# First layer of a two-layer adaLN model: retention in the planned instruction order, in groups of four batches with a choice of tokens each

## The chip, the cores and the metric

The kernel runs on one core of a Trainium2 chip (trn2). The metric is the device time of one execution in microseconds (us). A core has five engines that each take their instructions in program order: PE (TensorE, matrix products; PEld is its weight load), DVE (VectorE), ACT (ScalarE, with tables for its functions), POOL (GpSimd) and SP (SyncE, which here only issues DMA transfers; ACT and POOL issue some too). They meet through semaphores. Tensors lie in on-chip memory of 128 partitions; products go to PSUM, eight banks of 128 x 512 f32. All arithmetic here is in f32.

## What is computed

Input x is 16 batches of 256 tokens with 128 channels. Each of two layers has an attention-like part and a mixture of experts, each modulated by vectors that come from `silu(c) @ wmod`:

```python
h = layernorm(x) * (1 + ca) + sa
x = x + ga * retention(h)        # layer 0; layer 1: selective scan, then layer norm
h = layernorm(x) * (1 + cb) + sb
x = x + gb * experts(h)          # layer 0: experts choose tokens; layer 1: tokens choose 2 of 8
```

Retention has 8 heads of 16 channels with one decay each: a state `S = g*S + k v^T` and outputs `q S` over the 256 tokens, a group norm over each head and all tokens, weight and bias, and a projection `Wo`. The experts of layer 0 choose: a softmax over 8 experts for each token, then for each batch and expert the 64 tokens of highest probability; two products (128 to 512, exact gelu, 512 to 128), times the probability, added back to the tokens. Layer 1 has a selective scan with 256 inner channels and 16 states each, and then experts of width 448 in which a token goes to its best two.

## The kernel before

**Front, in Tile's own order (L334 to L713).** Tile is the layer that allocates tiles, puts in the waits, and here also orders the instructions of each engine. `attention(g)` (L418 to L494) takes batches 4g to 4g+3: layer norm of the inputs (`ln_stats` L334 with a Sqrt on ACT L344 and a reciprocal on DVE L345, `ln_apply` L349 on DVE), a transpose and modulation to hT, q and k with heads split in even and odd (ke, ko), v, the state S of the first 128 tokens, and scores in four PSUM banks of the pool `ps_sc`, four heads' rows each (L470). DVE multiplies each bank by the decay matrix into `pr0` to `pr3`, two buffers each (L472); PE forms the outputs from them (L481, L485), ACT copies them to yT, DVE takes their statistics (L493). `finish_attention(g)` (L496 to L528) does the group norm: two small products that average over a head, Sqrt, reciprocal, the normalized yn on DVE with its bias added on POOL (L521, L522), the projection, gate, and sum into X (L528). `gate(g)` (L530 to L545) normalizes X and forms the scores of the experts for all tokens. The calls are `attention(0)`, setup of layer 1's weights (L550 to L672), then for each g `attention(g+1)`, `finish_attention(g)`, `gate(g)`. After group 3 one choice serves all 16 batches (L681 to L713): softmax; the transpose to rows, one for each batch and expert, 128 in all; eight rounds of `max` and `match_replace`, eight tokens each (L700, L701); a running sum that numbers the chosen tokens; a write of these rows to memory (`spd`, L709); and a transpose back to `slot_tok`.

**The rest, in a planned order.** The class `Plan` holds chains of instructions, each with an urgency (a smaller number goes first), and prices of instructions. Its `issue` goes through a simulated time of its own, takes for each engine what could begin first (within 0.15 us, the most urgent), and binds the order with dependences between successive instructions of an engine. Chains name what they `need` and tokens that they `take` and `give` (buffers). All of these instructions are recorded under L115. Experts of layer 0 go by quarters q of four batches: `gather(b)` (urgency -10+q; builds one-hot matrices gg from slot_tok, px gathers tokens), `hidden(q)` (-8+q; ph, then gelu to hg), `outputs(q)` (-9+q; pye, ysb) and `scatter(q)` (-9+q; reads the rows of spd back, spread over partitions, as gt and pr, makes weights gt from them, pos adds back to X). q = 0 uses for ph four PSUM banks (dA0, dA1, c, y) that the scans use later. Layer 1 follows: `front(b)` (-16), `gates(b)` (-14), `scans()`, `back(k)` (-15), and `second()`, which plans the experts of layer 1, once all batches have left layer 0. `scans` works in 256 units of 128 x 512: `rep` rows come back from memory (dd) spread over partitions by SP, three buffers; ACT makes dA, POOL makes dB (twelve buffers), DVE scans into h and multiplies into dB, PE sums. Its chains have urgency -20 but for DVE's, 5. The experts of layer 1 (`expert` L1338 on, products pa and pg in L1372, py in L1402; sl is formed on DVE) go in tiles.

The memory of the retention (`p0`, `at`) is released before the pools `ml` (rep, dB) and `rf` (layer 0's experts) are opened.

Of the kernel before, what the change touches and what calls it, by code (L numbers as in the profile page):

```python
# [18 lines left out]
P = 128  # L19
# [239 lines left out]
def adaln_two_layers(ctx: ExitStack, tc: tile.TileContext, a: dict, out: bass.AP):  # L259
# [7 lines left out]

    def fixed32(pool, shape, name):
        return pool.tile(shape, U32, tag=name, name=name)
# [11 lines left out]
    early = ExitStack()  # L281
    pe = early.enter_context(tc.tile_pool(name="pe", bufs=1))
    pk0 = fixed(pe, [P, 554], "pk0")
# [13 lines left out]
    def w0(k):  # L297
        return pk0[:, PK0[k][0] : PK0[k][1]]

# [3 lines left out]
    with tc.tile_pool(name="su", bufs=1) as su, tc.tile_pool(name="sups", bufs=2, space=PSUM) as sups:  # L303
# [4 lines left out]
        nc.scalar.activation(sc.rearrange("p l b -> p (l b)"), w0("c"), AF.Silu)  # L308
# [20 lines left out]


# [3 lines left out]
    def ln_stats(srcs, rs=None):  # L334
        n = len(srcs)
        st = sm.tile([P, n, 6], F32, tag=f"st{n}", name="st")
        mv = sm.tile([P, n, 2], F32, tag=f"mv{n}", name="mv")
        sd = sm.tile([P, n], F32, tag=f"sd{n}", name="sd")
        rs = sm.tile([P, n], F32, tag=f"rs{n}", name="rs") if rs is None else rs
        for i, s in enumerate(srcs):  # L340
            nc.vector.bn_stats(st[:, i, :], s)
        for i in range(n):
            nc.vector.bn_aggr(mv[:, i, :], st[:, i, :])
        nc.scalar.activation(sd, mv[:, :, 1], AF.Sqrt, bias=eps5)  # L344
        nc.vector.reciprocal(rs, sd)  # L345
        return mv, rs

    def ln_apply(o, s, mv, rs, i):
        nc.vector.tensor_scalar(o, s, mv[:, i, 0:1], rs[:, i : i + 1], ALU.subtract, ALU.mult)  # L349

    def modulate(o, s, l, which, b):

        nc.scalar.activation(
            o, s, AF.Identity,
            bias=mods[l][:, 2 * which, b : b + 1], scale=mods[l][:, 2 * which + 1, b : b + 1],
        )

# [3 lines left out]

# [7 lines left out]
    spd = dr.tile([P, 2 * L], F32, tag="spd", name="spd", bufs=1)  # L369
# [3 lines left out]
    with tc.tile_pool(name="p0", bufs=1) as p0:  # L373
        c0 = fixed(p0, [P, 1536], "c0")
        eo = fixed(p0, [P, 2], "eo")
        nc.scalar.dma_start(c0, a["c0"][:, 0:1536])
        nc.scalar.dma_start(eo, a["c0"][:, 1600:1602])
        nc.scalar.dma_start(iota0, a["c0"][:, 1536:1600])
        nc.scalar.dma_start(lcol, a["c0"][:, 1602:1603])
        for b in range(4, B):  # L380
            nc.sync.dma_start(X[b], xsrc[b])
        nc.sync.dma_start(fw1, a["fw1"].rearrange("p (e h) -> p e h", e=E))
        nc.sync.dma_start(fw2, a["fw2"].rearrange("p (e h c) -> p e h c", e=E, h=4))

        def k0(k):
            return c0[:, C0[k][0] : C0[k][1]]

        dec = k0("dec").rearrange("p (j n) -> p j n", j=4)
        even, odd = eo[:, 0:1], eo[:, 1:2]


        wveo = fixed(p0, [P, 2, D], "wveo")
        nc.gpsimd.memset(wveo, 0.0)
        wv4 = w0("wv").rearrange("p (j q e) -> p j q e", q=2, e=DH)
        for par in range(2):
            nc.gpsimd.tensor_copy(
                wveo[:, par, :].rearrange("p (j q e) -> p j q e", q=2, e=DH)[:, :, par, :], wv4[:, :, par, :]
            )

        with tc.tile_pool(name="su1", bufs=1) as su1, tc.tile_pool(name="at", bufs=2) as at, tc.tile_pool(name="yt", bufs=8) as ytp, tc.tile_pool(  # L400
            name="ps_sc", bufs=4, space=PSUM
        ) as ps_sc, tc.tile_pool(name="ps_w", bufs=3, space=PSUM) as ps_w, tc.tile_pool(
            name="ps_g", bufs=1, space=PSUM
        ) as ps_g:
            p_tok = at.tile([P, NCH, B, E], F32, tag="p_tok", name="p_tok", bufs=1)
            gs = ps_g.tile([P, NCH, B, E], F32, tag="gs", name="gs")

            def transposed(xn, l, which, b, name):
                pt = ps_w.tile([P, 512], F32, tag="w", name=f"ptr_{name}{b}")
                for ch in range(NCH):  # L410
                    nc.tensor.transpose(pt[:, ch * P : (ch + 1) * P], xn[:, ch, :], ident)
                hT = at.tile([P, L], F32, tag="hT", name=f"hT_{name}{b}")
                modulate(hT, pt[:, :L], l, which, b)
                return hT

            yTs, gst, tabs = {}, {}, {}

            def attention(g):  # L418

                bs = range(4 * g, 4 * g + 4)  # L420
                tabs[g] = at.tile([P, 4, D], F32, tag="tab0", name=f"tab0_{g}")
                nc.sync.dma_start(tabs[g], rowd0[4 * g : 4 * g + 4, 0:D].unsqueeze(0).to_broadcast([P, 4, D]))
                mv, rs = ln_stats([X[b][:, ch, :] for b in bs for ch in range(NCH)])
                gst[g] = sm.tile([P, 4, 2], F32, tag="gst", name=f"gst{g}")
                for i, b in enumerate(bs):
                    xn = at.tile([P, NCH, D], F32, tag="xna", name=f"xna{b}")
                    for ch in range(NCH):
                        ln_apply(xn[:, ch, :], X[b][:, ch, :], mv, rs, NCH * i + ch)
                    hT = transposed(xn, 0, 0, b, "a")
                    pqk = ps_w.tile([P, 2, L], F32, tag="w", name=f"pqk{b}")  # L430
                    nc.tensor.matmul(pqk[:, 0, :], w0("wq"), hT, start=True, stop=True)
                    nc.tensor.matmul(pqk[:, 1, :], w0("wk"), hT, start=True, stop=True)
                    q = at.tile([P, L], F32, tag="q", name=f"q{b}")
                    ke = at.tile([P, L], F32, tag="ke", name=f"ke{b}")
                    ko = at.tile([P, L], F32, tag="ko", name=f"ko{b}")
                    nc.scalar.copy(q, pqk[:, 0, :])  # L436
                    nc.vector.tensor_scalar(ke, pqk[:, 1, :], even, None, ALU.mult)
                    nc.scalar.activation(ko, pqk[:, 1, :], AF.Copy, scale=odd)
                    qd = at.tile([P, P], F32, tag="qd", name=f"qd{b}")
                    nc.gpsimd.tensor_tensor(qd, q[:, P:L], k0("qdec"), ALU.mult)  # L440

                    pv = ps_w.tile([P, NCH, 2 * D], F32, tag="w", name=f"pv{b}")
                    for ch in range(NCH):
                        nc.tensor.matmul(
                            pv[:, ch, :], hT[:, ch * P : (ch + 1) * P], wveo.rearrange("p q d -> p (q d)"),
                            start=True, stop=True,
                        )
                    v = at.tile([P, NCH, 2 * D], F32, tag="v", name=f"v{b}")
# [107 lines left out]
            def k1(k):  # L556
                return pk1[:, PK1[k][0] : PK1[k][1]]
# [1004 lines left out]
```

## Time and profile before

| what | value |
|---|---|
| median of 3 runs | 1448.89 us (1442.01 to 1449.62) |
| profiled execution, its own time | 1455.8 us, clock 0.833 |
| its span | 1453.8 us, 19595 instructions |
| busy: PE, DVE, ACT, POOL | 1042.1 (72%), 921.6 (63%), 732.0 (50%), 729.3 (50%) us |
| first and last scan | 384.9 and 1198.8 us |
| chain that ended last, by engine | PE 32%, DVE 25%, ACT 14%, issue 9%, POOL 9%, DMA 6% |

How to read the views: the slices cut the span in 40 equal parts (36 us) with the busy share of an engine in tenths, and PEclk, the clock granted to PE. A table by stretch has the stretch, its length, then for PE, PEld, DVE, ACT and POOL the busy us with the number of records, then the granted clock, the share of DMA and GB/s. The lines of waits say which engine and tile waited for which, with the us in total, the number of times, and the longest. A group of one tile's instructions gives the shortest, median and longest duration in ns, and the first and the last start. The chain goes back from the last instruction, at each step to what released it; its lines are start, us, what. "<-" stands between output and inputs of an instruction, or between a waiting instruction and what it waited for.

### The profile page before, as it was taken

The numbers are of one execution on the slowest core, as the hardware profiler recorded it, in microseconds if no ns is written. First come the engines' busy times: TensorE is split into PE (matmuls) and PEld (weight loads), VectorE is DVE, ScalarE is ACT, GpSimd is POOL, SyncE is SP. The second block draws the span as 40 slices with busy tenths as digits, with TensorE's granted clock in tenths as the row PEclk, the third lists the DMA queues.
The fourth block names the chain that finished last, engine by engine and source line by source line (L and its number), as shares of the span: only waits on it lengthen the run. The fifth ranks groups of instructions, "written<-read, shape, count | busy, mean of one in ns | idle before, by whom it ended". The sixth has DMA issues, their size and how long they took to land.

```text
span 1453.8 us, 19595 instructions
## 1 busy us (share of the span) xinstructions
PE 1042.1 (72%) x6090; PEld 708.8 (49%) x6090; DVE 921.6 (63%) x1783; ACT 732.0 (50%) x1538; POOL 729.3 (50%) x1062
## 2 busy tenths in 40 slices
PE   5897795598878786768745576587627788778780
PEld 3575574386646554445423244254414455556560
DVE  3555555532497989888968688878926883423340
ACT  1222121333678977867655466767514654334441
POOL 0002203001566866757877787858673872322535
PEclk9996886699998988998965697778869979889895
DMA  7060000324345834476483343454323531112322
GB/s 255 6 169 8 9 1 0 76 48 109 102 116 143 192 87 137 110 159 167 131 235 110 102 128 92 104 131 118 93 83 89 125 94 44 36 46 53 80 64 54
DMA packets 105429, 142.01 MB, mean 98 GB/s; under 512 B 15560, under 2 KB 83584, under 8 KB 104704
## 3 DMA queue, kind: packets, MB, share of 16 engines
q1 hardware_dynamic: 99792, 124.84, 33.0%
q0 software_dynamic: 4256, 9.18, 2.3%
q10 hardware_dynamic: 1280, 6.74, 1.6%
q8 instruction: 51, 0.84, 0.3%
q14 instruction: 50, 0.41, 0.1%
HBM read 114.60 MB, written 26.12 MB: 97 GB/s over the span
## 4 chain that ended last, share of the span: by engine, by line
PE 32%; DVE 25%; ACT 14%; issue 9%; POOL 9%; DMA 6%; SPq 2%; another core or an unknown queue 2%; DVEq 0%; POOLq 0%; ACTq 0%
DVE h L115 10%; DVE dB L115 5%; PE py L1402 4%; ACT L115 4%; PE pa L1372 3%; ACT dA L115 3%; PE pg L1372 3%; POOL dB L115 3%; PE pxs L115 2%; PE pm L115 2%; DVE pr L472 2%; PE pye L115 2%; DVE sl L115 2%; DMA rep<-dd 2%; PE ph L115 2%
## 5 line engine op out<-in xcount | busy, mean ns | idle before, releaser
L115 POOL TENSOR_TENSOR dB<-rep,bt 128x512 f32<-128x512 f32 x256 | 327.7, 1303 | 149.6 <-DMA rep<-dd 96.3
L115 DVE TENSOR_TENSOR_SCAN h<-dA,dB 128x512 f32<-128x512 f32 x256 | 314.6, 1229 | 54.4 <-ACT dA L115 33.3
L115 ACT ACTIVATE dA<-rep,A 128x255 f32<-128x255 f32 x512 | 241.4, 476 | 149.5 <-DVE h L115 138.3
L115 DVE TENSOR_TENSOR dB<-h,ct 128x512 f32<-128x512 f32 x256 | 176.1, 688 | 6.5
L1402 PE MATMUL py<-w,mT 112*128 x680 | 102.3, 298 | 36.0 <-ACT mT L115 19.2
L115 DVE SCALAR_TENSOR_TENSOR sl<-sl,pa 128x448 f32<-128x448 f32 x85 | 52.4, 616 | 119.3 <-ACT sl L115 101.4
L1402 PEld LDWEIGHTS py<-w,mT 112*128 112x128 f32 x680 | 92.6, 206 | 64.9 <-issue 30.7
L1372 PE MATMUL pa<-w,xT 128*128 x170 | 93.0, 632 | 37.5 <-issue 19.1
L115 POOL DMA_INDIRECT got<-ydr,pos x64 | 61.4, 960 | 106.7 <-DMA xt<-disp 53.2
L115 PE MATMUL ya<-dB,c 128*32 128x512 f32 x512 | 82.4, 763 | 39.8 <-DVE dB L115 39.8
L115 ACT ACT_TABLE_LOAD x70 | 89.8, 1283 | 2.1 <-issue 0.9
L1372 PE MATMUL pg<-w,xT 128*128 x170 | 86.8, 595 | 2.7 <-DVE sl L115 1.0
L440 POOL TENSOR_TENSOR qd<-q,c 128x128 f32<-128x128 f32 x16 | 7.3, 457 | 159.2 <-ACT q L436 148.3
L115 PE MATMUL ph<-xin,fw 128*128 128x256 f32 x256 | 70.2, 417 | 23.6 <-DVE ysb L115 8.1
L1323 POOL DMA_INDIRECT disp<-hs,pos x64 | 61.9, 968 | 40.9 <-DVE pos L115 22.4
L115 ACT ACTIVATE yt<-py 128x128 f32<-128x128 f32 x85 | 23.3, 274 | 105.2 <-PE py L1402 52.5
L115 PE MATMUL pxs<-hTm,wcv 128*128 128x256 f32 x256 | 76.0, 445 | 0.0
L115 ACT COPY mT<-pm 112x512 f32<-112x512 f32 x85 | 49.3, 584 | 46.7 <-PE pm L115 33.6
L115 PE MATMUL pye<-fw,hg 128*64 128x128 f32 x1024 | 66.8, 283 | 6.0 <-ACT hg L115 5.9
L115 PE MATMUL pm<-c,sl 128*112 128x128 f32 x340 | 59.3, 299 | 14.0 <-issue 7.9
L115 PEld LDWEIGHTS ph<-xin,fw 128*128 128x128 f32 x256 | 50.4, 207 | 38.4 <-ACT xin L115 9.0
L115 PEld LDWEIGHTS pye<-fw,hg 128*64 128x64 f32 x1024 | 59.0, 141 | 19.2 <-ACT hg L115 8.3
(284 smaller groups left out, 2155.6 us busy)
## 6 DMA issues: line engine op xcount, KB each, us to landing
rep<-dd SPq DMA_DIRECT2D x128, 512.0 KB
gt<-spd SPq DMA_DIRECT2D x32, 256.0 KB
pr<-spd SPq DMA_DIRECT2D x32, 256.0 KB
dd<-dx SPq DMA_DIRECT2D x16, 512.0 KB
xt<-disp SPq DMA_DIRECT2D x85, 64.0 KB
ydr<-yt SPq DMA_DIRECT2D x85, 64.0 KB
w<-in_w ACTq DMA_DIRECT2D x3, 1792.0 KB
fw<-in_fw SPq DMA_DIRECT2D x2, 2048.0 KB
```

The lines of the kernel that those rows point to most:

```text
L115: return plan.op(key, us, lambda: getattr(real, name)(*args, **kw), lag)
L440: nc.gpsimd.tensor_tensor(qd, q[:, P:L], k0("qdec"), ALU.mult)
L472: nc.vector.tensor_tensor(prj.rearrange("p c q t -> p c (q t)"), psj.rearrange("p c q t -> p c (q t)"), dec[:, j, :].unsqueeze(1).to_broad ...
L1323: i = nc.gpsimd.indirect_dma_start(out=disp[g], out_offset=bass.IndirectOffsetOnAxis(ap=pos[g][:, c, r, :], axis=0), in_=hss[GROUPS[g][c / ...
L1372: nc.tensor.matmul(o, xT, w[:, bass.ds(which[0], 1), :].rearrange("p o i -> p (o i)"), start=True, stop=True)
L1402: nc.tensor.matmul(py, mT[:, ic, :], w2[:, bass.ds(which[0], 1), ic, :].rearrange("p o d -> p (o d)"), start=(ic == 0), stop=(ic == NFC - 1),)
```

## The change

- `retention(g)` takes the place of `attention`, `finish_attention`, `gate` and the single choice. It is written in the plan's chains: urgency -15+g/4 for norm, scores and outputs of four batches, one less for group norm, projection and expert scores, two less for `choose`.
- Each group has its own `choose()`, on 32 rows (4 batches x 8 experts) of 256, with a memory tensor `spd[g]` of its own.
- The scales of the norms come from `inv_std`, three Newton steps on POOL, in place of Sqrt and reciprocal; the norms themselves (xn, yn) are ACT activations with a scale and a bias.
- The scores use the banks dA0, dA1, c and y, one each, and one buffer each of `pr0` to `pr3`; `hidden(0)` uses the same banks.
- The retention's tiles (pool `at`) lie where `ml` lies later: `begin()`, which opens `ml` and plans `scans` and `back`, is called once `("slot", 3)` is planned. The experts of quarter q are planned once `("slot", q)`, the setup and the ph of q-1 are. Their pool `rf` opens in place of `pe` and `su1`. Fronts and gates are planned from the start.
- Urgencies of the experts: gather -15.5 (q=0) and -13.5+q/10, hidden -14.5 and -12.5+q/10, outputs and scatter -16.5 and -14.5+q/10.
- Buffers: xnq 1 for 2, gt 3 for 4, hg 2 for 3.
- c0 and eo are issued on ACT early; fw1 and fw2 move from SP to ACT after the first norm; the loads of X[4:] come ahead of rowd0; the setup of layer 1's weights is one planned chain (-15.2).

The diff, cut to its core:

```diff
-            prj = at.tile([P, NCH, 2, P], F32, tag=f"pr{j}", name=f"pr{b}_{j}")
+                prj = prs[b, j] = at.tile([P, NCH, 2, P], F32, tag=f"pr{j}", name=f"pr{b}_{j}", bufs=1)
...
+    pl.tokens(hTa=4, an=8, xna=2, q=2, v=2, kd=1, pr0=1, pr1=1, pr2=1, pr3=1, yT=6, tabA=4, yn=2, res=1)
-    pl.tokens(xin=4, xnq=2, gg=2, gt=4, pr=1, hg=3, ysb=4, fres=1, tab0=1, fn=2)
+    pl.tokens(xin=4, xnq=1, gg=2, gt=3, pr=1, hg=2, ysb=4, fres=1, tab0=1, fn=2)
...
+        own = ((ps_d, "dA0", "va"), (ps_d, "dA1", "vg"), (ps_c, "c", "vx"), (ps_y, "y", "vy"))
+        up = -15 + g / 4
...
+            for j in range(4):
+                pl.chain(up + b / 100)
+                need(("qk", b), *([("pr", b - 1, j)] if b > first else []))
+                ...
+                take(f"pr{j}")
+                take(tok)
...
+        def group_norm(g):
+            pl.chain(up - 1)
+            need(*(("yst", 4 * g + i) for i in range(4)))
+            ...
+            rs = inv_std(vv, 1e-5, 4, f"y{g}")
...
+        def choose():
+            pl.chain(up - 2)
+            need(*(("gs", base + i) for i in range(4)))
+            n, rows = NCH * 4, 4 * E
+            ...
+            for r in range(CAP // 8):
+                m8 = sm.tile([rows, 8], F32, tag="m8", name=f"m8_{g}_{r}", bufs=2)
+                V.max(m8, work[r % 2], us=0.43)
+                V.match_replace(work[(r + 1) % 2], m8, work[r % 2], -1.0, us=0.45)
+            ...
+            Q.dma_start(spd[g], sp.rearrange("p i t -> p (i t)"))
+            ...
+            done(("slot", g))
+
+        norm(g)
+        for i in range(4):
+            scores(base + i)
+            outputs0(base + i)
+        group_norm(g)
+        for i in range(4):
+            project(base + i)
+        expert_scores(g)
+        choose()
+
+    pl.chain(-20)
+    need(("an", 0))
+    S.dma_start(fw1, a["fw1"].rearrange("p (e h) -> p e h", e=E), us=0.35)
+    S.dma_start(fw2, a["fw2"].rearrange("p (e h c) -> p e h c", e=E, h=4), us=0.35)
...
-        pl.chain(-10 + q)
+        pl.chain((-13.5 if q else -15.5) + q / 10)
-        pl.chain(-8 + q)
+        pl.chain((-12.5 if q else -14.5) + q / 10)
-            pl.chain(-9 + q)
+            pl.chain((-14.5 if q else -16.5) + q / 10)
...
+    def experts_of(q):
+        nonlocal rf
+        if not q:
+            phase.close()
+            rf = first_layer.enter_context(tc.tile_pool(name="rf", bufs=1, side="right", reuse_waits="tile"))
+        for b in range(4 * q, 4 * q + 4):
+            gather(b)
         hidden(q)
         outputs(q)
         scatter(q)
+
+    def begin():
+        nonlocal ml
+        before.close()
+        ml = ctx.enter_context(tc.tile_pool(name="ml", bufs=2, reuse_waits="tile"))
+        scans()
+        for k in range(NB):
+            back(k)
+
+    for g in range(4):
+        retention(g)
     for b in range(B):
         front(b)
         gates(b)
-    scans()
-    for k in range(NB):
-        back(k)
+    pl.after([("slot", 3)], begin)
+    for q in range(4):
+        pl.after([("slot", q), "setup"] + ([("ph", q - 1, E - 1)] if q else []), lambda q=q: experts_of(q))
     pl.after([("x0", b) for b in range(B)], second)
```

## The prediction

> **What bounds the kernel now.** I read the slices of the page first, to see where engines are idle; then the view of the scans, for where the long stage begins and ends; then the table of busy time by stretch for what lies before it; then the waits and the chain there.
>
> ```profile
> PE   5897795598878786768745576587627788778780
> DVE  3555555532497989888968688878926883423340
> PEclk9996886699998988998965697778869979889895
> ```
> ```profile
> L115 DVE TENSOR_TENSOR_SCAN h<-dA,dB x256: 1195/1231/1232, 384.9 to 1198.8; 128x512 f32<-128x512 f32 x128
> ```
> A slice is 36 us. DVE is loaded to 8 or 9 tenths only from slice 11 on: that is the stage of the 256 scans, 384.9 to 1200 us. What comes before it is 385 us in which PE leads, and what comes after is 254 us of the last experts. So there are three lengths, and the change rewrites the first.
>
> ```profile
> core 0: us, PE busy (x) PEld busy (x) DVE busy (x) ACT busy (x) POOL busy (x), PEclk, DMA share, GB/s
> 30.00:80.00 50.00, 42.65 (x347) 31.58 (x347) 26.19 (x78) 10.96 (x23) 1.83 (x4) 0.86 0.22 47
> 80.00:107.00 27.00, 26.25 (x268) 20.12 (x268) 13.79 (x31) 6.82 (x15) 1.37 (x3) 1.00 0.57 153
> 107.00:135.00 28.00, 17.44 (x95) 13.73 (x94) 15.62 (x71) 7.20 (x15) 6.95 (x9) 0.62 0.03 10
> 164.00:192.00 28.00, 18.96 (x112) 15.15 (x110) 15.98 (x71) 4.18 (x10) 7.26 (x9) 0.63 0.04 11
> 228.00:262.00 34.00, 20.06 (x82) 17.07 (x80) 16.87 (x75) 6.98 (x13) 11.61 (x14) 0.50 0.00 1
> 262.00:276.00 14.00, 1.37 (x5) 0.66 (x5) 11.55 (x34) 0.37 (x1) 0.00 (x0) 0.50 0.05 19
> 276.00:289.00 13.00, 10.29 (x18) 3.83 (x19) 5.66 (x8) 5.07 (x9) 0.00 (x0) 0.82 0.66 159
> 289.00:324.00 35.00, 35.00 (x345) 29.04 (x344) 10.43 (x14) 15.03 (x27) 0.00 (x0) 1.00 0.27 62
> 335.00:385.00 50.00, 41.16 (x273) 31.02 (x272) 10.85 (x25) 21.33 (x37) 13.16 (x26) 0.93 0.54 132
> ```
> Two kinds of stretch alternate. In 80:107 (scores) and 289:324 (experts) PE is full at clock 1.00. In 107:135, 164:192 and 228:262 (group norm, projection and gating of one group) it does 17 to 20 us of work in 28 to 34, at half to 0.63 of the clock, and in 262:276 the choice of tokens leaves it 1.37 us. PE's work from 30 to 385 sums to 285 us of 355, part of it at the low clock. The waits of the retention say why:
>
> ```profile
> POOL yn L522 <- DVE yn L521: 35.0, 4, 9.5
> PEld po L525 <- POOL yn L522: 20.8, 12, 3.9
> PE ptr_f L411 <- DVE xnf L349: 14.2, 4, 3.6
> DVE pr L472 <- PE sc L470: 10.7, 17, 2.0
> ```
> PE waits for small chains over DVE, POOL and ACT while nothing else is ready for it. After the choice the chain goes through memory:
> ```profile
> 273.87 2.00 DMA spd<-sp
> 277.89 5.74 DMA pr<-spd
> ```
> So the front is PE work with holes, and filling the holes is what can be won.
>
> **What the Trainium skill says.** "TensorE: Matmul & The Clock Gate", Part 1, says that PE's clock is halved or full according to how busy PE has been: the table agrees (0.50 in 228:262, 1.00 in 289:324), so a filled hole also speeds the work around it. "Perfetto Trace Analysis", section on the Tensor Engine instruction, says that ACT, DVE and GpSimd are strict first-in first-out; the records agree, since the reciprocal of the second group's norm (L345, 20.26) holds up all of DVE behind it. Here this makes the planner's order binding. "DMA: Bandwidth & Descriptors", Issuing engines are not separate DMA queues, says that transfers of all issuers share the same 16 engines; before, c0 and eo, issued at 15.17 and 15.54 right behind 4 MB of expert weights from SP, land only at 26.8 and 29.5. "ScalarE: Activation LUTs", What ACT_TABLE_LOAD costs, gives 1283 ns a load, as does the trace (mean of 70: 1283). The built programs hold 75 loads each, so removing the eight Sqrt calls wins none of these: I count nothing.
>
> **The change, part by part** (profiled execution: 1455.8 us, span 1453.8; the median of the runs is 0.5% lower, 1448.9).
>
> *Start.* c0 is issued before the silu and eo right after it, ahead of the weights. The first scores come at 30.07, after "DVE ke <- DMA eo". Without that wait: statistics of four batches are done at 9.4; the new norm scale takes 16 small POOL operations, which in this trace stand 0.284 us apart (336.75 to 341.3), 4.6 us; two ACT normalizations of some 0.48, a transpose, hT 0.56, pqk and q as now (15.0 to 18.1, 3.1) make about 19. Gain 11. The cover: weights land some 16 us after their issue in either order and are wanted only after 80.
>
> *PE work up to the last scores.* At full clock: 16 batches x 8.5 us (the four `pr` products of a batch start at 81.00, 89.53, 98.05) = 136; projection and gating 16 x 1.9 = 30; of the experts before the first scan px 17.7, ph 28.8, pye 26.3, pos 7.8 (by tile, 276 to 385); two fronts 22; setup 5. Sum 273 less rounding of shared pieces, I take 270, the same in both: the instruction order of both builds has both quarters' ph, all of q0 and about half of q1's pye, and two fronts ahead of the first scan. In the changed order, what follows the last retention output py15 is ph x26 of 58 (12.9), pye x71 of 199 (9.4), the last six px (6.6), two groups' gating (10), po and transposes (5): 44. So 226 lies before it, and there the group norms and choices of one group are now covered by scores of the next and by experts. Not covered: choice 0, with nothing to run but the scores of group 1 (8, an estimate: about half of the 14.5 that the one choice leaves PE idle now), choice 1 (6), waits for gt transfers on DVE ("DVE gt <- DMA pr<-spd" is 18.8 for five now; I take 8). Single-buffered `pr0..3` and score banks make PE wait for DVE within a batch: at least nothing, at most 0.69 x 4 a batch = 44; the plan puts other work between, and I take 7.5% of 226 = 17 (80:107 misses 0.75 of 27, 3%, with two buffers; my estimate is over double that). End of retention outputs: 19 + 226 + 22 + 17 = 284.
>
> *The serial end.* From py15 DVE's order has the group norm of group 3, then all of choice 2, then statistics, softmax and choice 3, then the first scan. Group norm 3.0, its 17 POOL operations 4.8, yn, po, res and X of four batches 4; choice 2 in between on DVE 10 (8 pairs of max and match_replace took most of the 11.55 of DVE in 262:276); statistics 3; inv_std 4.6; gating of four batches 5; softmax 5; choice 3 11; slot_tok 1; rep by DMA 5 (377.0 to 381.5) and dB 1.3. Sum 58. `begin` admits the scan rows only after slot 3, since they lie in the retention's memory, so none of it is skipped. That the change does not do what it says (experts beside retention) is excluded by the same order: all of q0 stands ahead of py15. First scan at 342 against 384.9: **-43**. The 44 us of PE work fit beside these 58.
>
> *POOL.* Twelve calls of inv_std add 12 x 4.6 = 54 us, and yn's 16 additions leave; POOL is under 12 us busy in every stretch before 335, so only the calls inside the serial end count, and they are counted. *ACT* gets 64 normalizations (31 us) and 16 yn (8): 97 us busy of 355 now, so cover is wide.
>
> *Scan stage.* On DVE between the first and last scan the changed order has sl 60 for 68, acc 4 for 8, gt 9 for 8, spd 14 for 15: 8 x 0.62 + 4 x 0.4 + 0.7 - 1.3 = 6 less. The stage is DVE-bound (83% busy), so **-6**. Those four expert tiles go to the tail, where PE sets the pace: a tile, which has two sl, costs 3.3 to 3.9 us there (20 sl from 1310 to 1343; 36 from 1349 to 1420): 4 x 3.5 = **+14**. SP: gt and pr transfers stand between reps in either order; with three gt buffers for four I take nothing, the bound is rival C.
>
> Sum -43 - 6 + 14 = -35: 1420.8, and 0.5% lower for the median: **1414**.
>
> **Rivals.** *A, full packing.* None of the 17 of inefficiency, and 7 of the 10 of choice 2 done before py15: first scan near 318, 24 less: 1396.8, median 1390. For it: PE was at 1.00 whenever it was fed. Against: strict order on DVE. *B, gain eaten.* The planner's prices are guesses, and a misjudged DMA or chain stalls an engine that holds work for all others. If PE's holes stay as now in half the places (10 us for each of three group ends) the first scan falls at 372: 1450.8, median 1444. For it: the 20.8 us of "PEld po <- POOL yn" are such a wait, with only one group to fill it. *C, slower.* A gt transfer on SP waits until a buffer is free, and all later rep transfers wait behind it. Now 12 dB rows cover 12 x 1.92 (1229 + 688 ns) = 23 us. POOL already lost 96.3 us of idle time to "DMA rep<-dd", with four buffers. If a gt is held over 23 us, the excess stops the scans; nine stand in the stage, and 6 us each cost 54: 1472, median 1466.
>
> **How the numbers follow.** Forecast 0.57 (1398 to 1432: 16 either way for the 17 and 22 of stalls), A 0.10, B 0.15, C 0.18. 0.5%, about what a measurement here can tell from no change, is 1441.7 to 1456. B falls one third on the faster side: faster 0.72, same 0.10, slower 0.18. The range goes from A to just past B, 1388 to 1447, and leaves out C and slivers.
>
> **What would show it.** First `pr` near 21; `yst15` near 284; first scan near 342, last near 1150; PE clock over 0.9 from 40 to 280; tail 14 longer. C shows as "POOL dB <- DMA rep" well over 96 us. The prediction is wrong if the first scan is later than 375 or the scan stage is over 830.

## The result and the profile after

The changed kernel takes 1466.88 us (median of 4 runs, 1460.31 to 1468.69) beside 1449.26 for the kernel before: 1.0116 times, with a 95% interval of 1.0078 to 1.0154. The forecast was 1414. A later control (e14) gave 1.017 (1.0151 to 1.0188).

The profiled execution has a span of 1458.5 us. From its page, the slices of PE and DVE and PE's clock:

```profile
PE   5997799868665867677652467867627788688880
DVE  3566615444898799887986869878817875233330
PEclk9987999878778998789885679878859699899895
```
DVE's full slices begin one slice (36 us) earlier than before, at the 11th of 40 for the 12th. At the other end nothing has moved forward: the last low slices, the tail, are as many as before. The view of the scans of the changed kernel gives the three lengths:

```profile
L115 DVE TENSOR_TENSOR_SCAN h<-dA,dB x256: 1197/1232/1232, 359.2 to 1186.1; 128x512 f32<-128x512 f32 x128
```
The first scan comes 26 us earlier (384.9 before), the last only 13 (1198.8), and the end is 5 us later in span. The busy table of the changed kernel (columns as before: PE, PEld, DVE, ACT, POOL, clock, DMA share, GB/s):

```profile
30.00:282.00 252.00, 231.23 (x1888) 175.44 (x1887) 134.47 (x403) 98.00 (x207) 56.85 (x184) 0.90 0.25 62
164.00:192.00 28.00, 21.01 (x137) 15.14 (x138) 15.86 (x46) 11.04 (x23) 0.46 (x1) 0.88 0.08 22
228.00:262.00 34.00, 32.86 (x245) 24.36 (x243) 18.58 (x50) 15.49 (x31) 11.32 (x41) 0.95 0.43 101
282.00:320.00 38.00, 26.01 (x102) 17.74 (x104) 19.96 (x72) 15.75 (x28) 12.74 (x27) 0.71 0.04 16
320.00:359.00 39.00, 33.33 (x244) 27.09 (x240) 12.25 (x42) 15.97 (x29) 5.73 (x17) 0.76 0.18 43
```
The largest hole of the retention is filled as meant: 228:262 has 32.86 us of PE work at clock 0.95, for 20.06 at 0.50 before. The one at 164:192 is not: 21.01 us for 18.96, though at clock 0.88 for 0.63. Up to the last outputs, 30 to 282, PE is idle for 21 of 252 us. What is left open is mostly the end, 282 to 359.

The profiles of one kernel differ by up to 12 us between executions (the kernel before: spans of 1453.8 and 1441.9; changed: 1458.5 and 1470.0), so terms are read below from the controls e14 and e15, taken together, as well. Runs that were not taken together differ as a whole: beside e1 to e4 and e13 to e16 the kernel before takes about 1449, beside e17 and e18 1445, beside e5 to e12 1409. Times are therefore told as ratios to the kernel before in the same set of runs. Even so, the ratio of the changed kernel, with nothing altered in it, went from 1.0116 to 1.017 between two sets, so ratios of different sets carry about half a per cent of doubt beyond their intervals.

| run | ratio, 95% | first scan | stage | tail | sl in the stage |
|---|---|---|---|---|---|
| before (e15) | 1 | 386.9 | 806.8 | 248.2 | 68 |
| changed (e14) | 1.017 (1.0151 to 1.0188) | 360.4 | 836.8 | 272.8 | 60 |
| e1 weights on SP | 1.0091 (1.0064 to 1.0118) | 353.1 | 834.0 | 272.4 | 60 |
| e2 before, few buffers | 1.0237 (1.0202 to 1.0273) | 392.1 | 826.3 | 259.9 | 64 |
| e3 sums first | 0.9942 (0.9908 to 0.9976) | 364.6 | 815.7 | 259.6 | 68 |
| e4 not beside | 1.036 (1.0306 to 1.0415) | 388.2 | 818.2 | 291.9 | 54 |
| e5 buffers back* | 0.9942 (0.9905 to 0.998) | 360.0 | 803.2 | 230.0 | 66 |
| e6 before, sums first* | 1.0316 (1.0271 to 1.0362) | 386.8 | 819.9 | 243.4 | 60 |
| e7 before, gt 3* | 1.0185 (1.0141 to 1.023) | 388.9 | 804.3 | 236.1 | 64 |
| e8 before, hg 2* | 1.0142 (1.0093 to 1.0192) | 388.2 | 801.5 | 240.3 | 62 |
| e9 before, price* | 1.0118 (1.009 to 1.0146) | 385.5 | 788.7 | 234.8 | 64 |
| e10 changed, price* | 0.9951 (0.9929 to 0.9974) | 373.7 | 795.1 | 231.9 | 68 |
| e11 before, slack* | 1.0017 (0.9994 to 1.004) | | | | 64 |
| e12 changed, slack* | 1.0089 (1.0061 to 1.0117) | 372.4 | 800.7 | 246.0 | 60 |
| e13 tiles held | 1.0054 (1.0033 to 1.0075) | 381.9 | 807.0 | 270.2 | 60 |
| e16 buffers and order | 0.9944 (0.9925 to 0.9964) | 367.3 | 827.6 | 240.7 | 74 |
| e17 late scans | 1.0282 (1.0226 to 1.0337) | 386.3 | 823.3 | 271.2 | 60 |
| e18 all three | 0.9962 (0.9929 to 0.9995) | 378.1 | 807.5 | 259.7 | 66 |

First scan, stage (first to last scan) and tail (last scan to the end of the span) are us from one profile each; * marks the sets in which the kernel before took 1409; the profiled execution of e11 was a slow one (1421.3 us, median of the others 1409.5), so its lengths are left out. Sl counts DVE's instructions on tiles of layer 1's experts: two sl make one expert tile; what the stage does not hold is left for the tail.

### The profile page after: what moved, and what is told of

Same layout as the page of the kernel before. It is cut to its first block, busy times and chain, and to the rows that moved or that the text cites. A ratio compares the mean times of both kernels' runs of the same rounds, so it can differ in the third digit from the quotient of the medians.

```text
span 1458.5 us, 19912 instructions
## 1 busy us (share of the span) xinstructions
PE 1042.0 (71%) x6104; PEld 707.2 (48%) x6104; DVE 931.0 (64%) x1803; ACT 764.1 (52%) x1612; POOL 756.2 (52%) x1241
## 4 chain that ended last, share of the span: by engine, by line
PE 35%; DVE 25%; POOL 13%; ACT 11%; issue 8%; DMA 5%; another core or an unknown queue 3%; DVEq 0%; SPq 0%; POOLq 0%; ACTq 0%
DVE h L115 9%; PE py L1485 4%; DVE dB L115 4%; PE pa L1455 4%; POOL dB L115 4%; PE pg L1455 3%; DMA rep<-dd 3%; ACT dA L115 3%; PE pxs L115 3%; ACT L115 2%; PE sc L115 2%; PE ph L115 2%; PE ya L115 2%; PE pm L115 2%
## 5 line engine op out<-in xcount | busy, mean ns | idle before, releaser
L115 DVE TENSOR_TENSOR_SCAN h<-dA,dB 128x512 f32<-128x512 f32 x256 | 314.9, 1230 | 66.9 <-ACT dA L115 39.4
L115 PE MATMUL ph<-xin,fw 128*128 128x256 f32 x256 | 73.3, 430 | 16.4 <-ACT hg L115 6.2
L115 PE MATMUL pye<-fw,hg 128*64 128x128 f32 x1024 | 69.9, 293 | 11.2 <-ACT hg L115 7.7
L115 PEld LDWEIGHTS pye<-fw,hg 128*64 128x64 f32 x1024 | 62.7, 147 | 19.4 <-ACT hg L115 9.4
L115 PE MATMUL px<-gg,xnq 128*128 128x512 f32 x64 | 44.2, 818 | 37.3 <-DVE gg L115 37.3
```

The costliest lines, as they stand in the source:

```text
L115: return plan.op(key, us, lambda: getattr(real, name)(*args, **kw), lag)
```

## The experiments

**e1, the weights' issue.** In the changed kernel ACT's own records at the start are:

```profile
10.81 10.40 ACTq L115 DMA_DIRECT2D fw<-in_fw  x2
21.31 1.65 ACT L115 ACTIVATE xna<-x,nb_a,iy_a 128x128 f32<-128x128 f32 x4 [16.82 <-DMA lcol<-in_c]
```
In the order that was built the two issues stand ahead of the first normalization, whose scale POOL had ready at 16.3. The first line merges two records. Apart they read:

```profile
L115 ACTq DMA_DIRECT2D fw<-in_fw x2: 334/334/335, 10.8 to 20.9; - x2
```
Each issue takes 0.33 us, but the second begins 10 us after the first. Its record in the trace carries a wait for a semaphore that it shares with a load of x: SP issued that load at 13.12, and its landing is told at 20.85 (in e14 the second issue starts at 21.74, after a landing at 21.72). "DMA: Bandwidth & Descriptors" of the Trainium skill, Issuing engines are not separate DMA queues, calls an issuing sequencer's time usually small beside the transfer; the trace agrees with 0.33 us. What held ACT for 10 us was this wait, not the work of issuing, so the 10.4 us that the expectation below puts on the issues is a misreading, though the place of the loss is right.

```diff
-    S.dma_start(fw1, ...)
-    S.dma_start(fw2, ...)
+    Q.dma_start(fw1, ...)
+    Q.dma_start(fw2, ...)
```


> The changed kernel, with the two loads of the expert weights (fw1, fw2) issued by SP behind its small loads instead of by ACT ahead of the first normalization; the order of DVE is the same. In the changed kernel ACT spends 10.4 us on these two issues (10.81 to 21.2) and its first normalization starts at 21.31. My theory: retention is a chain of full PE work from its first scores on, so the first pr goes from 30.7 to about 24.5, the first scan from 359.2 to about 353, and the time falls by 4 to 6 us, to about 1462. Rival: the stage of the scans and the tail set the end whatever the front does, and the time stays at 1467 within 2. Second rival: the weights land too late for the small transfers behind them on SP (tabA of group 0), and the first group norm waits: first scan not earlier.

Measured: the normalization began at 16.98 and the first pr at 25.6 (30.7 in the changed kernel), the last retention output came at 281.3 (282.0), the first scan at 353.1, the last at 1187.1 (1186.1). On SP the two issues started at 47.1 and 47.7. The time, 1462.13, is the one that the first theory named, but 1.0091 against 1.0116 cannot be told apart and the last scan came no earlier. The retention absorbed the five us at the start, and the stage absorbed the six at the first scan.

**e2, e7, e8, the buffers, taken from the kernel before.**

```diff
-    pl.tokens(xin=4, xnq=2, gg=2, gt=4, pr=1, hg=3, ...)
+    pl.tokens(xin=4, xnq=1, gg=2, gt=3, pr=1, hg=2, ...)   # e2; e7: gt=3 alone; e8: hg=2 alone
```


> The kernel before, with the smaller numbers of buffers of the changed kernel for layer 0's experts (xnq 1 for 2, gt 3 for 4, hg 2 for 3), nothing else. Theory that the buffers give back the gain in the stage of the scans (rep transfers held behind gt on SP): the stage grows from 814 by 10 or more and the time goes to 1460 or above, with POOL's idle time for rep rising from 96 towards 150. Theory that the order of the layer-1 experts does it: the first scan is later by less than 4, the stage keeps its length within 4, and only the two expert tiles that this order puts in the tail rather than the stage (64 sl for 68) cost some 7: about 1455.

> The kernel before with three gt buffers for four and the others as they were. If the transfers of gt on SP, ahead of rep, are what the smaller numbers cost: most of the 33 us, 1475 or above, with POOL idle for rep at 115 or more. If the third hg is what counts (gelu of one expert beside the products of another): within 8 of 1450.

> The kernel before with two hg buffers for three and the others as they were. If hg is what counts: 1475 or above, the first scan 5 to 7 later (experts of q0 and q1 stand alone in front of it) and the stage 10 longer. If gt is: within 8 of 1450, but for up to 10 us of tail from 62 sl in the stage for 68.

All three cost 2.4%, gt alone 1.9%, hg alone 1.4%. Neither single one was "the" buffer, and POOL's idle time for rep rose only from 96 to 118 in e2. After e2 I believed the buffers to be the cause, and gave them back:

**e5, the buffers back** (from quarter 2 on, in memory that is free once the retention's tiles are gone).

```diff
-            gt = gts[b] = rf.tile(..., tag="gt", bufs=3)
+            gt_ = "gtx" if q > 1 and b % 4 == 3 else "gt"
+            gt = gts[b] = (rx if gt_ == "gtx" else rf).tile(..., tag=gt_, bufs=1 if gt_ == "gtx" else 3)
```
(and so for hg and xnq, with a token each.)

> The changed kernel, with the buffers of before given back from quarter 2 on (a fourth gt, a third hg, a second xnq, in the memory that stays free once the retention's tiles are released); nothing else. Taking these buffers from the kernel before cost 33 us (1450 to 1483: 7 at the first scan, 12 in the stage, 4 in the tail of the profiles). Theory that the buffers are the main loss of the change: the first scan stays at 359 within 3, the stage shrinks from 827 to about 815, the tail by 10 (66 sl in the stage for 60), and the time is about 1445. Theory that only the number of expert tiles in the stage matters: stage unchanged, tail 10 shorter, 1456. Rival, that the stage of the changed kernel is held by something else: within 4 of 1467.

0.9942: it beats both kernels, the one before by 0.6%. But this edit also gave the planner another order (66 sl), as e2, e7 and e8 did (64, 64, 62). Buffers and order are mixed in all four.

**e3 and e6, one urgency, on both kernels.**

```diff
-        pl.chain(<urgency of scatter>)   # the chain of pos, fres and the sum into X
+        pl.chain(-21)
```


> The changed kernel, with the chain that adds the experts of layer 0 back to X (pos, fres, the sum on POOL) at urgency -21, ahead of the scans' rows on POOL at -20; nothing else. The built order ends layer 0 at scan 95 instead of 124 and has 68 sl in the stage again instead of 60. Theory that the tail is longer because four expert tiles were left for it: the tail shrinks by 14 (271 to 257) and the time falls to about 1453. Rival, that the stage itself is slowed by contention or waits for rep: the stage stays at 827 or grows by the 5 us of DVE work that four tiles bring, and the time falls by less than 6. Second rival: ahead of dB on POOL these sums wait for the experts and starve the scans, stage over 840.

> The kernel before, with the same single edit that made the changed kernel 25 us faster (the chain that adds layer 0's experts to X at urgency -21); nothing else. Theory that this edit mends what the change had worsened (layer 0's last sums stood late on POOL, four expert tiles in the tail): the kernel before gains nothing, and as its built order has 60 sl in the stage for 68 it loses up to 14: 1450 to 1464. Rival, that the edit is a gain of its own that any such kernel would have: about 1425, and then the change itself still costs some 17 beside it.

The edit makes the changed kernel 1.7% faster (tail 272.4 to 259.6, stage 826.9 to 815.7) and the kernel before 3.2% slower. It is no gain of its own. What it has in common with the run before it: more sl in the stage where faster, fewer where slower.

**e9 to e12, draws of the order.** A draw is here one order out of the many that the planner could find. Nothing in these differs but a number in the planner's own arithmetic.

```diff
-            ... ALU.is_equal, us=1.0,      # price of gg; e9 on before, e10 on the changed kernel
+            ... ALU.is_equal, us=1.1,
-    SLACK = 0.15                           # e11 on before, e12 on the changed kernel
+    SLACK = 0.16
```


> The kernel before, with nothing changed but one price in the plan: the one-hot matrices gg count 1.1 us instead of 1.0 in the planner's own time. No buffer, wait or operation differs; only the order that the planner finds (64 sl in the stage for 68). Theory that the planner's order as such is worth one to three per cent and that the order before is a lucky draw: 1.01 to 1.03 times the time of the kernel before. Theory that buffers and waits, not the draw, decide: within 0.5%, but for 7 us of two more tiles in the tail.

> The changed kernel, with the same single price changed (gg 1.1 for 1.0): its built order has 68 sl in the stage instead of 60 and prepares layer 1's experts at scan 130 instead of 141, with the same few buffers. Theory of the draw: 1.2% or more faster than the changed kernel, 0.985 to 1.00 times the kernel before, and faster than the kernel before with the same price. Theory that the smaller buffers hold the stage: still 1.005 to 1.012 times the kernel before.

> The kernel before, with the planner's SLACK 0.16 us for 0.15 and nothing else: a second draw of the order, with the same places of gt and x0 up to scan 123 and 64 sl in the stage for 68. Draw theory: 1.005 to 1.02 times the kernel before, with the tail 7 longer. Otherwise within 0.5%.

> The changed kernel, with SLACK 0.16 for 0.15: 60 sl in the stage as in the changed kernel, but layer 1's experts prepared at scan 124 instead of 141. If the number of tiles that the stage holds sets the tail: within 0.5% of the changed kernel (1.007 to 1.017 times the kernel before). If the start of the preparation counts: 1% faster than it.

A price 0.1 us higher costs the kernel before 1.2% and turns the changed kernel from slower into faster than before. SLACK does nothing that can be measured to the one and leaves the other slow. e12 prepares layer 1's experts 17 scans earlier than the changed kernel; it cannot be told from the first measurement of that kernel (1.0089 and 1.0116), but is 0.8% faster than the control e14, so whether this start counts stays open. e9 also shrinks the reading of e2 and e7: their 2.4 and 1.9% lie only partly above a plain draw.

The number of tiles alone does not set the time either. With 64 sl in the stage the kernel before took 1.0017, 1.0118, 1.0185 and 1.0237 (e11, e9, e7, e2), and orders with 60 sl run from 1.0054 to 1.0316.

**e13, tiles alone.** From e10, the last four of the layer-1 tiles that stood between the scans wait for the last scan; DVE's order is otherwise the same up to the first of them.

```diff
         pl.chain(-12 + g + j / 100)
+        if g == 1 and j >= 7:
+            need(("scan", 255))
```


> The changed kernel with the price of e10 (68 sl in the stage, 0.995 of the kernel before), but with the last four of the expert tiles of layer 1 that stood between the scans made to wait for the last scan: 60 sl as in the changed kernel, and the order of DVE is the same up to the first of these tiles. Theory that tiles left for the tail are what makes the changed kernel slow: the stage shrinks by at most 4 x 1.3 = 5 us, the tail grows by 4 x 3.5 = 14, and the time goes from 0.995 to 1.002 to 1.006. Stronger form: to 1.010 or above, all of the difference. Rival, that it was only a mark of something else in the order (waits in the stage): within 0.3% of e10.

From 0.9951 to 1.0054, each against the kernel before in its own set: four tiles in the tail rather than between the scans cost 1.0%, 15 us. In the records DVE's order of the two runs is the same up to 1148 us of e10, 21 us before its last scan. That held tiles cost time is shown; the size is less sure, since the two ratios come from different sets.

**e4, nothing beside retention.**

```diff
-        pl.after([("slot", q), "setup"] + ..., lambda q=q: experts_of(q))
+        pl.after([("slot", 3), "setup"] + ..., lambda q=q: experts_of(q))
```


> The changed kernel, with the experts of layer 0 planned only after the last group's choice, so that none runs beside retention; nothing else. If experts beside retention are what brings the first scan forward: the retention ends near 282 - 70 = 212 to 230, the choice of group 3 near 290, then 75 us of experts of q0 and fronts stand alone, and the first scan falls at 375 to 390; with 54 sl in the stage the tail grows by another 10, and the time is 1485 to 1500. If running beside brings little, because both want PE: first scan within 8 of 359, time within 8 of 1467.

As the first theory had it: first scan 388.2, tail 291.9 with 54 sl, 1.036. The experts beside retention do bring the first scan forward by about 29 us. Without them it comes no earlier than in the kernel before (384.9), so in this run the whole gain at the first scan is theirs.

**e14 and e15, controls.**

> The changed kernel unchanged, as a control. Its ratio should be 1.008 to 1.015 again; first scan near 359, stage 10 to 15 longer than that of the kernel before on this chip, tail 14 to 17 longer.

> The kernel before unchanged, for its profile on the chip of the other three: first scan near 385; if this chip is the one of the later runs, a stage of some 790 and a tail of 235 instead of 814 and 255.

By these two the first scan gains 26.5, the stage loses 30.0 and the tail 24.6: stage and tail lose more than I expected of the control, and the stage, 836.8, passes the 830 that the prediction named as a sign of being wrong (826.9 in the first profile). By batches of 16 scans, the lead of the changed kernel is 26.5 at batch 0, 20 at batch 1, 23 at batch 2, 10 at batch 3, 4 at batch 4 and nothing at batch 5 (612.7 against 612.4). So in this pair the gain is lost within five batches, and the views of that stretch must show it. (In the first pair of profiles 16 of 26 us are lost there: the lead is 9.4 at batch 5 and 12.7 at the last scan.) Busy times and DVE's waits, the kernel before (e15):

```profile
386.90:612.40 225.50, 169.75 (x1018) 113.20 (x1018) 197.17 (x247) 183.80 (x325) 155.14 (x171) 0.90 0.51 128
```
```profile
DVE h L115 <- ACT dA L115: 16.8, 11, 3.6
DVE h L115 <- POOL nb_o L115: 2.6, 1, 2.6
DVE u L115 <- ACT thu L115: 2.6, 1, 2.6
```
The changed kernel (e14):

```profile
360.40:612.70 252.30, 175.44 (x966) 116.78 (x970) 204.32 (x250) 170.75 (x307) 148.13 (x159) 0.80 0.52 125
```
```profile
DVE h L115 <- ACT dA L115: 18.4, 9, 8.5
DVE gt L115 <- DMA pr<-spd: 10.6, 3, 6.3
DVE sz L115 <- ACT thz L115: 5.6, 1, 5.6
DVE u L115 <- ACT thu L115: 5.4, 3, 2.6
DVE st_o L115 <- PE pom L115: 3.6, 1, 3.6
DVE yg L115 <- PE ya L115: 1.8, 1, 1.8
```
DVE is busy 7 us more (seven gt there for four, and slower gg) and idle 48.0 for 28.3. The waits of the scans themselves hardly differ; new are waits of what stands between scans in DVE's fixed order: weights gt of layer 0's experts, and pieces of the next fronts. In the records of DVE for e14 it looks so:

```profile
461.54 1.23 DVE L115 TENSOR_TENSOR_SCAN h<-dA,dB 128x512 f32<-128x512 f32 x1
469.08 1.28 DVE L115 SCALAR_TENSOR_TENSOR gt<-gt,lcol,pr 128x1024 f32<-128x1024 f32 x1 [6.31 <-DMA pr<-spd]
...
471.48 1.22 DVE L115 TENSOR_TENSOR_SCAN h<-dA,dB 128x512 f32<-128x512 f32 x1
478.32 0.69 DVE L115 SCALAR_TENSOR_TENSOR sz<-thz,pz 128x512 f32<-128x512 f32 x1 [5.62 <-ACT thz L115]
```
Two scans in 18 us (the next starts at 479.71), because an instruction ahead of the next one waits. SP, meanwhile, waits for PE's pos to free a gt buffer:

```profile
SPq L115 <- PE pos L115: 14.0, 2, 7.1
```
The first profile of the changed kernel, over the same five batches, tells which of this comes back:

```profile
359.20:601.30 242.10, 165.25 (x961) 109.95 (x962) 207.91 (x249) 168.85 (x305) 150.49 (x160) 0.85 0.54 131
```
```profile
DVE h L115 <- ACT dA L115: 19.4, 10, 8.4
DVE sz L115 <- ACT thz L115: 6.0, 1, 6.0
DVE gt L115 <- DMA pr<-spd: 2.2, 2, 2.0
```
DVE's extra work (207.9 us for 197.2 before) and the wait of sz are there again; the wait for gt is 2.2 us, not 10.6. So gt's wait varies from one execution to the next and is not the cause as such. A rival that no run separates is PE's clock in these batches: 0.90 before, 0.80 and 0.85 in the changed kernel, with PE's results among what DVE waits for.

**e17, the early start taken away.** A hundred small statistics on DVE ahead of the first scan, without a price, so that all orders stay.

```diff
+        late = sm.tile([P, 6], F32, tag="late", name="late", bufs=1)
+        for _ in range(100):
+            V.bn_stats(late, X[0][:, 0, :], us=0.0)
```


> The changed kernel with 100 small statistics of DVE (some 0.2 us each, about 20 us in all, written to a tile that nobody reads) put ahead of the first scan, at no price in the plan, so that the order of every engine is that of the changed kernel but for these. If the early first scan is worth nothing in this order, because what DVE holds between the scans of the first five batches is not ready sooner: first scan at about 380, stage 15 to 20 shorter, last scan within 5 of the changed kernel's, and 1.012 to 1.019 of the kernel before, as the changed kernel (1.012 and 1.017). If the stage is a fixed length of DVE work: the end moves by the whole 20 us, 1.026 to 1.031.

They took 33 us, not 20 (99 of them in 32.52, 0.33 each), and the first scan came 26 later than in e14 and 27 later than in the first profile, where the kernel before has it. The early start is not worth nothing: the last scan came 12.4 later than in e14 and 23.5 later than in the first profile, and the ratio rose from 1.017 or 1.0116 to 1.0282, 16 or 24 us. Between half and nearly all of the shift reached the end, and the second theory is not excluded. What e17 does show is the cost of the order itself: from the same start as the kernel before, its stage is 823.3 us for 813.9 and 806.8, and already its first five batches take 239.9 for 225.8 and 225.5. So of the 13 to 30 us by which the stage of the changed kernel grew, some 9 to 17 are what this order costs in any case, and some 4 to 14 are a lead that the rest did not follow.

**e16 and e18, the parts together.**

```diff
 # e5 and e1, and
-    SLACK = 0.15
+    SLACK = 0.16        # e16; e18 also has the urgency of e3 and the price of e10
```


> The changed kernel with the buffers given back from quarter 2 on (e5), the weights issued by SP (e1), and SLACK 0.16: of five values it is the one whose built order holds most tiles in the stage, 74 sl for 60. If front, buffers and tiles add up: first scan near 355, the tail 7 x 3.5 = 24 shorter than the changed kernel's, stage as in e5: 0.978 to 0.986 of the kernel before. If the stage takes back what is put into it: no better than e5, 0.994.

> The changed kernel with buffers given back from quarter 2 on, weights issued by SP, the sums of layer 0 first (as e3), the gg price of e10 and SLACK 0.16: layer 0 ends at scan 89 in its order, 70 sl in the stage. If these add up: tail 17 shorter than the changed kernel's, 0.98 to 0.988 of the kernel before. If the stage takes it back as in e16: 0.994.

0.9944 and 0.9962. In e16 the tail shrinks with seven more tiles (272.8 to 240.7), but its first scan comes at 367.3 and its stage, 827.6, is still 21 us longer than that of the kernel before in the same set (806.8); nothing adds up beyond e3 and e5. (e18 holds 66 sl between its first and last scan, not 70.) The best versions (e3, e5, e10, e16) lie at 0.994 to 0.995 and cannot be told apart.

## Why the prediction was wrong

The forecast summed three terms to -35. In the first pair of profiles they came to -26 + 13 + 17 = +5 (its changed profile is the fastest of the four executions), in the controls to -26.5 + 30.0 + 24.6 = +28; the medians lie between, 17.6 apart. Had only the stage's term held at -6, the sum would still have been a gain, -14 and -8. The stage decides the sign.

**Start, 19 us: wrong, and without effect.** "The cover: weights land some 16 us after their issue in either order" looked at the landing and not at where the issues stand: moved to ACT, the second of them waits, and the first normalization behind it with it (10 us); the first pr came at 30.7 instead of 21. e1 shows that this did not decide.

**PE work up to the last outputs: right as a sum, by luck.** 284 was forecast, 282.0 measured, but two misses cancel: the first pr came 10 us late, and PE then stood idle for 21 us up to 282, where I had allowed 39 (22 and 17).

**The serial end, 58 us: took 77.** In DVE's records of the changed kernel:

```profile
282.44 0.18 DVE L115 BATCH_NORM_AGGREGATE gst<-yst 128x2 f32<-128x6 f32 x1
...
288.31 0.17 DVE L115 COPY p_tok<-gs 128x16 f32<-128x16 f32 x1 [2.71 <-PE gs L115]
288.40 0.77 DVE L115 COPY m<-gst 128x4 f32<-128x4 f32 x1
...
295.76 0.16 DVE L115 COPY vv<-pgm 128x4 f32<-128x4 f32 x1 [0.32 <-PE pgm L115]
...
307.50 0.42 DVE L115 TENSOR_TENSOR res<-po,tabA 128x256 f32<-128x256 f32 x1 [0.84 <-POOL x L115]
...
318.76 0.61 DVE L115 BATCH_NORM_AGGREGATE mv_g<-st_g 128x2 f32<-128x6 f32 x8
...
338.03 0.17 DVE L115 COPY p_tok<-gs 128x16 f32<-128x16 f32 x1 [5.23 <-PE gs L115]
...
350.44 0.23 DVE L115 COPY slot_tok<-psl 128x64 f32<-128x64 f32 x1
...
359.16 1.23 DVE L115 TENSOR_TENSOR_SCAN h<-dA,dB 128x512 f32<-128x512 f32 x1 [8.42 <-ACT dA L115]
```
Choice 2 took about the 10 I had, and the last choice 10 for 11. Wrong were the terms that I summed as if each chain stood alone: the group norm began 6 us late, behind p_tok copies of the group before that wait for PE; it took 7.4 for 3.0; gating four batches took 14 (324 to 338) for 5, since PE's queue holds ph and pye between them (eight ph, 3.3 us, from 332.44 on, ahead of the last gs); rep and dA took 8.5 for 6.3. So the first scan gained 26, not 43.

**Scan stage, -6: this step failed.** I took "The stage is DVE-bound (83% busy)" to mean that its length is the sum of DVE's instructions, so that it would start earlier and shrink by the four tiles' work. It grew by 13 (first pair) and 30 (controls). The stages of the kernel before and the changed kernel, first pair and then e15 and e14:

```profile
384.90:1198.80 813.90, 563.08 (x2936) 357.79 (x2933) 661.38 (x1032) 533.42 (x1097) 583.75 (x831) 0.82 0.48 124
359.20:1186.10 826.90, 539.69 (x2824) 340.79 (x2825) 661.92 (x1020) 521.13 (x1069) 573.07 (x821) 0.81 0.47 121
386.90:1193.70 806.80, 559.24 (x2935) 358.24 (x2932) 657.66 (x1031) 533.25 (x1097) 581.96 (x831) 0.81 0.49 125
360.40:1197.20 836.80, 552.90 (x2824) 349.22 (x2825) 659.64 (x1020) 521.52 (x1069) 570.77 (x821) 0.79 0.47 120
```
DVE's work did not shrink by 6: it is 661.4 and 661.9, 657.7 and 659.6, since the 5.8 and 6.1 us less of sl and acc came back as 8.8 and 6.9 us more of gg, gt and spd (one gt is added, the rest are slower). And the growth is idle time of DVE, 152.5 to 165.0 and 149.1 to 177.2, for which the forecast had no term. DVE was busy for 81% of the stage before, not 83%, and the remaining fifth is waits. DVE takes its list in a fixed order, with experts of layer 0 and fronts threaded in, and these were hardly sooner than before: the last sum of layer 0's experts on DVE starts at 723 and 737 us in the two profiles, for 728 and 729 before. By e17 the order costs 9 to 17 us in the stage, and a start 26 us earlier is worth 12 to 24 at the end. Which of DVE's waits is the root of the order's cost stays open.

**Tail, +14: right in kind, small in size.** Four tiles, 17 and 25 longer in the two pairs of profiles; e13 gives 15 us for four tiles moved alone. In the sets at about 1449 a tile is (271.8 - 240.7) / 7 = 4.4 us between 60 sl (mean of five tails) and 74, for my 3.5. I had the cost and did not ask what it rests on: how many tiles fit is decided by the planner, and e9 to e12 show that a change of a price moves the time as much as the whole change did.

**Rivals.** C had the sign, and its mark came true: POOL's wait for rep is well over the 96.3 us of before, in the changed kernel and then in e16:

```profile
POOL dB L115 <- DMA rep<-dd: 151.5, 36, 31.3
POOL dB L115 <- DMA rep<-dd: 154.6, 41, 31.7
```
But e16 is among the fastest, so the mark does not measure a cost, and the path was not the one I had: DVE hardly starved for dB (one wait of 4.8 us in the first profile, 3.5 in e14), and it waited for gt itself between 2.2 and 10.6 us in the first five batches, at most a fifth of the 54 I had priced. I put the buffers at nothing; whether they cost anything beyond the draw is not settled, since no run changes them and keeps the order. B's mechanism, a wait that the plan did not know of and that holds up a fixed order, is what happened at the start and in the stage.

**What the change is worth.** With the same edit on both, the changed kernel stands to the kernel before as 0.9951 / 1.0118 = 0.984 (price), 1.0089 / 1.0017 = 1.007 (slack), 0.9942 / 1.0316 = 0.964 (urgency), and 1.012 to 1.017 as given. (The first two pairs were taken together, the third was not.) In these four draws the sign is the draw's and not the change's. Open stays what the change would be worth over many draws, and why some draws hold more tiles than others.

## What to carry to other kernels

Where a list scheduler fixes the order, a change to one part draws a new order for all of it: perturb a price a little in both kernels (here by a tenth) before believing a difference of one or two per cent. An earlier start of a stage need not reach its end whole, where work threaded into that stage comes no earlier; look for waits of the threaded work, not of the stage's own. And count how much filler the long stage still holds, since what it no longer holds is paid at the end (about 15 us for four tiles in e13).

## What was not expected of the hardware

The same gg takes 0.68 us on DVE where POOL is idle and mostly over twice that beside POOL's dB; in the changed kernel:

```profile
292.24 0.68 DVE L115 TENSOR_TENSOR gg<-slot_tok,iota 128x512 f32<-128x512 f32 x1
...
403.17 3.06 DVE L115 TENSOR_TENSOR gg<-slot_tok,iota 128x512 f32<-128x512 f32 x2
```
Of the first profile's gg, ten ran with POOL idle (681 to 686 ns) and eight wholly or almost wholly beside dB (1384 to 1756); the scans took 1230 ns in either case. (Of a scan's inputs one, dA, lies in PSUM; both of gg's do not. Whether that is why they differ, no run tests.) It is not a fixed rule: in e14 one gg beside dB took 681. Its mean in the stage rose from 1192 to 1513 ns in the first pair, 5 us in sum, and from 1188 to 1335 in the controls, without any change to it.

And the kernel before took 1449 us in some sets and 1409 in others, with a mean granted clock of 0.836 and 0.843. The record names the same chip for e9 to e12 (1409) and e13 to e16 (1449), so that it is a matter of the chip is not shown; the cause stays open. Orders with as many tiles had both lengths shorter in the faster sets (e12 against the changed kernel, 60 sl: stage 800.7 for 827 to 837, tail 246.0 for 272); this is more than the changes studied here.
